# Head of an attention and spectral-convolution kernel: one load queue, other fillers, biases on ScalarE, keys of three blocks first, and the gate's means one step earlier

## The chip, the cores and the metric

The kernel runs on one core of a Trainium2 chip. The metric is the device time of one execution in microseconds (us). Three runs of the kernel before took 3039.53, 3043.44 and 3043.40 us; their median is 3043.4. A profile is one further execution, recorded by the hardware. The engines are named PE (TensorE; PEld is its weight load), DVE (VectorE), ACT (ScalarE), POOL (GpSimd) and SP (SyncE, which here only issues transfers).

## What is computed

The input x has four images of 64 channels and 96 x 96 pixels. Layer 0 is an attention over all 9216 pixels with a sigmoid in place of the softmax, followed by a channel gate; layer 1 mixes a few Fourier modes. Both stand behind a group normalisation and add to their input.

```python
q, k, v = wq @ g + bq, wk @ g + bk, wv @ g + bv      # g = _gn(x), 8, 8 and 64 channels
energy = einsum('bcn,bcm->bnm', q, k)
out = einsum('bcm,bnm->bcn', v, sigmoid(energy)) + g
scale = sigmoid(mlp(mean of out) + mlp(max of out))  # per image and channel
x = x + out * scale
x = x + irfft2(the 32 x 16 low modes of rfft2(_gn(x)), mixed over channels)
```

## The kernel before, in words

Two images share the 128 partitions, so there are two pairs of images, `x0` and `x1`, each a tile of 128 x 9216 numbers. A pair's pixels are cut into 18 blocks of 512. For each block of queries the kernel runs over 144 energy tiles of 128 x 512 (72 groups of 128 keys, two images). These are worked off in bursts of mostly seven: PE multiplies keys and queries into PSUM banks (`energies`, L531), ACT puts the sigmoid into one of two sets of seven slots of `at` (`sigmoids`, L552), and PE multiplies with the values into an accumulator bank (`attend`, L569). At the end of a block DVE adds the accumulator to x and takes its sum and maximum (L575, L577).

Before the first burst lies the head. Pair 0 is loaded in nine pieces of 1024 columns, 512 KB each, on the queues of SP (pieces 0, 2, 4, 6, 8) and ACT (1, 3, 5, 7), then constants and pair 1 follow on SP (L99 to L108). DVE takes statistics of each block (L583), aggregates them (L134), and a short chain over PE, DVE and POOL (`second` and `third` of `group_stats`, L136 to L149) gives the mean and the scale of each group. DVE normalises blocks 0 and 1 (L155). PE projects the keys of block 0 (L429), the queries (L519) and the values (L450). Keys and queries are split into a high part of fewer bits and a rest: DVE adds the bias out of PSUM (L435, L521), copies into the narrower type (L436, L522) and combines (L418). In between, `warm` (L622) issues products whose result nobody reads; some stand behind a statistic, some behind a projection.

What order the work has: in the head, a scheduler orders the instructions of each engine, with `issue_after` where an order is forced. From the first burst on, PE, ACT and DVE follow the program text (`manual_schedule`, L838). Which step stands beside which burst comes from a planner (L751 to L823): `together[t]` holds projections that share the banks of burst t + 1, `alone[t]` steps that stand by themselves, `ends[t]` steps for the end of burst t. Keys and values of later blocks of pair 0 are projected during the first bursts. A later block's query comes back from a copy of the split projections in DRAM (L493 stores, L510 loads, both on SP).

The last block of pair 0 has a crossing into the first block of pair 1. There, `second_layer(t)` (L676) plans layer 1 of pair 0, which runs beside the attention of pair 1. Its first step is the gate of pair 0: `means` (L598: three small DVE operations, L600 to L602, of which `f` comes out), `hidden` (L604: a PE product that reads `f`, L606) and `gates` (L609). Around the crossing the projections of pair 1 are made (`values_of(1, s)`), and their `rest` (L476) splits and turns queries and keys on DVE (L486, L487, L489).

Of the kernel before, what the change touches and what calls it, by code (L numbers as in the profile page):

```python
# [33 lines left out]
F32 = mybir.dt.float32  # L34
# [52 lines left out]
def tile_kernel(ctx: ExitStack, tc: tile.TileContext, x, cst, late, spec, out):  # L87
# [11 lines left out]
    for p in range(NPAIR):  # L99
        xt = xpool.tile([P, N], F32, tag=f"x{p}", name=f"x{p}")  # L100
        for s in range(9):
            cols = bass.ts(s, N // 9)
            queue = nc.scalar if p == 0 and s % 2 else nc.sync
            queue.dma_start(xt[:, cols], xf[bass.ts(p, P), cols])
        if p == 0:
            nc.sync.dma_start(cs[:, :NFIRST], cst[:, :NFIRST])
        xs.append(xt)
# [4 lines left out]
    def named(name, rows=P):  # L112
        return cs[:rows, PLACE[name]]
# [277 lines left out]
    with tc.tile_pool(name="work", bufs=1) as work, \  # L391
# [17 lines left out]
        def bank_a(name):  # L409
            return banks[:, spare[0], :]  # L410
# [5 lines left out]
        def low_or_high(dst, u, h, is_low):  # L416

            mark[0] = nc.vector.scalar_tensor_tensor(dst, h.bitcast(F32), is_low, u,  # L418
                                                     ALU.mult, ALU.add)

        def later(step):
            with tc.issue_after(mark[0].ins):
                step()

        def keys(p, s):
            pp = bank_a(f"pk_{p}_{s}")
            for e in range(2):
                cols = bass.ts(e, P // 2)
                projected[0] = nc.tensor.matmul(  # L429
                    pp[cols, :NB // 2], named("wk")[:, cols],  # L430
                    xs[p][:, bass.ts(2 * s + e, NB // 2)], start=True, stop=True)
            shape = [P, NB // 2]
            u = qp.tile(shape, F32, tag="turned", name=f"full_k_{p}_{s}")
            h = qp.tile(shape, F32R, tag="t", name=f"high_k_{p}_{s}", bufs=1)
            nc.vector.tensor_scalar(u, pp[:, :NB // 2], named("bk"), None, ALU.add)  # L435
            nc.vector.tensor_copy(h, u)  # L436
            low_or_high(kT[:, s, :, :], u.rearrange("p (m h) -> p h m", h=2),
                        h.rearrange("p (m h) -> p h m", h=2), low_sb[:, 1:2])

        def values_of(p, s, width=C + 2 * C8):  # L440


            pp = banks[:, spare[0]:spare[0] + 2, :].rearrange("p b (k m) -> p b k m", m=P)
            src = xs[p][:, bass.ts(s, NB)].rearrange("p (a m h) -> p a h m", a=2, h=2)
            for a in range(2):
                for h in range(2):
                    for e in range(2):
                        for b in range(2):
                            rows = bass.ts(b, C)
                            projected[0] = nc.tensor.matmul(  # L450
                                pp[bass.ts(e, P // 2), b, 2 * a + h, :width],
                                src[rows, a, h, bass.ts(e, P // 2)],
                                named("wv")[rows, :width], start=True, stop=True)

            def values():
                for b in range(2):
                    nc.vector.tensor_tensor(  # L457
                        vT[:, 4 * s:4 * s + 4, bass.ts(b, C)].rearrange(
                            "p (h a) m -> p a h m", h=2),
                        pp[:, b, :, :C].rearrange("p (a h) m -> p a h m", h=2),  # L460
                        named("bv")[:, :C].unsqueeze(1).unsqueeze(1).to_broadcast([P, 2, 2, C]),
                        ALU.add)

            if width == C:
                values()
                return None
            u = qp.tile([P, 2, 4, 2 * C8], F32, tag="u", name=f"u_{p}_{s}")
            nc.vector.tensor_tensor(
                u.rearrange("p b k o -> p (b k) o"),
                pp[:, :, :, C:width].rearrange("p b k o -> p (b k) o"),  # L470
                named("bqk").unsqueeze(1).to_broadcast([P, 8, 2 * C8]), ALU.add)
            values()

            k = 2 if p == 0 and s < DIRECT else 0

            def rest():  # L476
                t = qp.tile([P, 3, 2, 2, QK], F32R, tag="t", name=f"t_{p}_{s}", bufs=1)
                pieces = [(u[:, :, :, :C8],
                           t[:, 2].rearrange("p a h (b o l) -> p l b (a h) o", b=2, l=2))]
                if k == 0:  # L480
                    pieces += [(u[:, :, :, C8:].rearrange("p b k o -> p (b k) o").unsqueeze(3)
                                .to_broadcast([P, 8, C8, 2]),
                                t[:, :2].rearrange("p b a h (l o y) -> p l (b a h) o y",
                                                   l=2, y=2))]
                for whole, to in pieces:
                    nc.vector.tensor_copy(to[:, 0], whole)  # L486
                    nc.vector.tensor_tensor(to[:, 1], whole, to[:, 0].bitcast(F32), ALU.subtract)  # L487
                turned = qp.tile([P, 3, 2, NB // 8], F32, tag="turned", name=f"turned_{p}_{s}")
                nc.vector.transpose(  # L489
                    turned[:, k:].rearrange("p k a (m h) -> p (k a) h m", h=2),  # L490
                    t[:, k:].rearrange("p k a h m -> p (k a) h m").bitcast(F32))
# [23 lines left out]
        def first_queries():  # L515


            pq = bank_a("pq_first")
            projected[0] = nc.tensor.matmul(pq, named("wq"), xs[0][:, :NB], start=True, stop=True)  # L519
            qu, qh = at[:, 12, :], at[:, 13, :].bitcast(F32R)  # L520
            nc.vector.tensor_scalar(qu, pq, named("bq"), None, ALU.add)  # L521
            nc.vector.tensor_copy(qh, qu)  # L522
            q = qp.tile([P, NB], F32R, tag="q", name="q_first")
            low_or_high(q, qu, qh, low_sb[:, 0:1])
            return q

        def energies(t):

# [87 lines left out]

            return gate, [means, hidden, gates], f

        def warm(s, n=NB):


            return nc.tensor.matmul(banks[:, 7, :n], xs[0][:, s * NB:s * NB + P], xs[0][:, s * NB:s * NB + n],  # L622
                                    start=True, stop=True)

            if NBLK - 4 < s < NBLK:
                with tc.issue_after(last.ins):
                    warm(s, NB // 2)
        each, norm0, _ = stats_of(0)
        for s, step in enumerate(each):
            last = step()  # L630
            if s < NBLK:
                warm(s, NB // 2)
        with tc.issue_after(last.ins):
            warm(NBLK - 3)

        def warm_behind():
            with tc.issue_after(projected[0].ins):
                warm(NBLK - 1, NB // 2)

        norm0[0]()  # L640
        norm0[1]()
        spare[0] = 2
        keys(0, 0)
        warm_behind()
        spare[0] = 3
        q = first_queries()
        warm_behind()
        spare[0] = 0
        values_of(0, 0, C)
        warm_behind()  # L650

        together, alone, ends = {}, {}, {}

        def end(t, step):
            ends.setdefault(t, []).append(step)
# [20 lines left out]
        def second_layer(first):  # L676

            gate, steps, _ = after(0)
            end(first + 1, steps[0])
            for step in steps[1:]:  # L680
                follow(True, step, 2)
            l1 = Hidden(0, gate, bank_a, lambda dst, src: nc.vector.tensor_copy(dst, src), work)  # L682
# [46 lines left out]
        each, norm1, mv1 = stats_of(1)  # L729
        again = vT.rearrange("p j m -> p (j m)")  # L730
        kept = [TILES * (NPAIR * NBLK - 1) + 2 * (STRIP // P) * (s + 1) for s in range(NSTRIP)]
        ask, asked, known, valued, normal, renewed, again_at = {0: q}, 1, 2, 2, 3, 0, 0
        heads = [HEAD]
        sizes, total, order, done, block, edges = [5], [5], [[4, 5, 6, 3, 2]], [], [], set()
        way = 1
# [15 lines left out]
        while len(done) < len(sizes):  # L751
# [18 lines left out]
            elif total[t] < ALL:  # L770
# [2 lines left out]
                    steps.append((1, lambda s=known: keys(0, s)))  # L773
                    known += 1
                while (valued < min(NBLK, (total[t] + 5 * SIZE - 1) // 8 + 1)
                       and sum(n for n, _ in steps) <= 2):
                    steps.append((2, lambda s=valued: values_of(0, s)))
                    if valued >= DIRECT:
                        arrive(t, 0, valued)
                    valued += 1  # L780
# [47 lines left out]
        burst = [t for t, size in enumerate(sizes) for _ in range(size)]  # L828
        assert not chain and renewed == NBLK and asked == NPAIR * NBLK

        energies(0)
        sigmoids(0)
        later(norm0[2])
        spare[0] = 7
        keys(0, 1)
        spare[0] = 0
        values_of(0, 1)()
        with tc.manual_schedule(engines=ENGINES):  # L838
            put_off = []
            for t in range(T):  # L840
                if t + 1 < T:
# [305 lines left out]
```

## Time and profile before

| | |
|---|---|
| median of the runs | 3043.4 us |
| the profiled execution | 3040.91 us, of which the span of the trace is 3039.1 us |
| PE busy | 3014.8 us, 99% of the span |
| ACT busy | 2410.9 us, 79% |
| DVE busy | 309.0 us, 10% |
| first statistic starts, last one ends | 5.61 us, 17.11 us |
| first product of the mean chain (L138) starts | 17.84 us |
| first normalise starts | 20.39 us |
| first keys' product starts | 21.36 us |
| first energies start | 27.82 us |
| first sigmoid starts | 28.38 us |
| fourth burst's energies start | 41.46 us |
| queries of block 1 first used | 123.5 us |
| means of pair 0 (L600) start | 1494.95 us |

Times in the trace count from the span's start. In lines of a timeline the columns are start, length, engine, line of the program, operation, what is written and read, how many, and in brackets how long the engine stood idle before and what ended that. The lines of a table by stretches give, for each engine in turn (PE, PEld, DVE, ACT, POOL), its busy time and the number of instructions; then come the clock granted to PE as a share of full speed, the busy share of the DMA engines and the GB/s they moved. In the chain of work that ended last, each line is a start, a length and what ran.

### The profile page before, as it was taken

Reading aid. Unit: us, or ns where it says so; the run is one execution under the profiler, and the core shown is the slowest. Engines: PE = TensorE matmul, PEld = TensorE weight load, DVE = VectorE, ACT = ScalarE, POOL = GpSimd, SP = SyncE. Lnnn points to the kernel's source line nnn. Section 1 sums busy time; section 2 is a strip of 40 time slices with the busy share of each in tenths; the row PEclk is TensorE's granted clock in tenths of the full one; section 3 lists DMA queues with packets and bytes.
Section 4 is the critical chain, followed back from the end, with each engine's and each line's share of the span. In section 5 each row is a group of like instructions: output and inputs, shape, how many; then the busy total and the mean of one; then the engine's idle time right before and its main releaser. Section 6 shows DMA issues by size and latency. Waiting matters only on the chain.

```text
span 3039.1 us, 44084 instructions
## 1 busy us (share of the span) xinstructions
PE 3014.8 (99%) x19360; PEld 1112.5 (37%) x19360; DVE 309.0 (10%) x709; ACT 2410.9 (79%) x1541; POOL 75.5 (2%) x148
## 2 busy tenths in 40 slices
PE   8999999999999999999999999999999999999998
PEld 4333333333333333333333333333333333333335
DVE  6300000000000000002411101100000000000005
ACT  4788888888888888887788887777778888888872
POOL 0100000000000000001300000000001000000001
PEclk9999999999999999999999999999999999999999
DMA  4100000000000000001422322412113000000027
GB/s 158 32 4 4 4 4 4 4 4 4 1 4 4 4 4 4 4 4 34 95 68 67 87 78 86 134 33 45 52 45 121 4 4 4 4 4 5 5 62 252
DMA packets 114289, 117.34 MB, mean 39 GB/s; under 512 B 77520, under 2 KB 84432, under 8 KB 114000
## 3 DMA queue, kind: packets, MB, share of 16 engines
q1 hardware_dynamic: 103584, 86.20, 10.5%
q0 software_dynamic: 8848, 23.60, 2.4%
q10 hardware_dynamic: 1664, 4.72, 0.4%
q8 instruction: 152, 2.49, 0.3%
q14 instruction: 41, 0.34, 0.0%
HBM read 79.80 MB, written 33.49 MB: 37 GB/s over the span
## 4 chain that ended last, share of the span: by engine, by line
PE 97%; DVE 1%; DMA 1%; issue 0%; ACT 0%; POOL 0%; SPq 0%; DVEq 0%; POOLq 0%; ACTq 0%
PE banks L569 77%; PE banks L531 17%; PE banks L450 1%; PE banks L209 1%; PE pv L209 0%; DMA x<-in_x_dram 0%; PE pa L947 0%; DVE x L1052 0%; PE banks L382 0%; ACT at L552 0%; PE banks L429 0%; PE pu L959 0%; PE banks L305 0%; DMA vt<-vd 0%; PE pz L1031 0%
## 5 line engine op out<-in xcount | busy, mean ns | idle before, releaser
L552 ACT ACTIVATE at<-banks 128x2048 f32<-128x2048 f32 (+1 forms) x1501 | 2388.4, 1642 | 558.7 <-PE banks L531 543.9
L569 PE MATMUL banks<-at,vT 128*64 128x512 f32 (+1 forms) x11824 | 2400.8, 547 | 0.0
L569 PEld LDWEIGHTS banks<-at,vT 128*64 128x64 f32 x11824 | 778.3, 136 | 1361.5 <-issue 1306.5
L531 PE MATMUL banks<-q,kT 32*128 32x512 f32 x5040 | 541.8, 452 | 0.8 <-ACT at L552 0.7
L531 PEld LDWEIGHTS banks<-q,kT 32*128 32x128 f32 x5040 | 223.7, 183 | 446.3 <-issue 339.2
L575 DVE SCALAR_TENSOR_TENSOR x<-banks,x 128x512 f32<-128x512 f32 x36 | 24.9, 691 | 2022.0 <-PE banks L569 2022.0
L502 POOL DMA_DIRECT2D stage<-qk x96 | 47.6, 503 | 934.4 <-DMA qk<-turned 925.5
L386 DVE TENSOR_TENSOR x<-banks,x 128x768 f32<-128x768 f32 x12 | 11.5, 957 | 168.8 <-PE banks L382 153.2
L450 PEld LDWEIGHTS banks<-cs,x 64*64 64x64 f32 x1152 | 21.8, 135 | 16.2 <-ACT at L552 11.5
L457 DVE TENSOR_TENSOR vT<-banks,cs 128x256 f32<-128x256 f32 x72 | 26.8, 413 | 0.0
L450 PE MATMUL banks<-cs,x 64*64 64x80 f32 (+1 forms) x1152 | 25.9, 234 | 0.0
L577 DVE TENSOR_REDUCE maxs<-x 128x1 f32<-128x512 f32 x36 | 24.6, 684 | 1.2
L149 POOL TENSOR_TENSOR mr_l<-ve_l,cs 128x1 f32<-128x1 f32 x4 | 2.2, 561 | 841.1 <-DVE ve_l L148 841.1
L583 DVE BATCH_NORM_STATS2 stats<-x 128x6 f32<-128x512 f32 x36 | 22.2, 679 | 6.0 <-DMA x<-in_x_dram 5.9
L682 DVE COPY ws<-banks 128x512 f32<-128x512 f32 x16 | 11.1, 691 | 115.3 <-PE banks L209 115.3
L622 PE MATMUL banks<-x 128*128 128x256 f32 (+1 forms) x44 | 15.0, 486 | 6.3 <-DMA x<-in_x_dram 6.2
L682 DVE COPY ae<-banks 128x512 f32<-128x512 f32 x6 | 4.1, 692 | 157.6 <-issue 115.3
L932 POOL DMA_DIRECT2D x<-vT x3 | 2.7, 990 | 660.0 <-DVE less L922 660.0
L531 PE MATMUL banks<-q_first,kT 32*128 32x512 f32 x144 | 18.0, 459 | 0.9 <-ACT at L552 0.5
L489 DVE STREAM_TRANSPOSE turned<-t 128x384 f32<-128x384 f32 (+1 forms) x35 | 17.8, 510 | 1.2
L947 PE MATMUL pa<-xt,lc 128*128 128x256 f32 x72 | 16.9, 386 | 1.1 <-DVE xt L939 1.1
L155 DVE TENSOR_SCALAR x<-x,mr_l 128x512 f32<-128x512 f32 x36 | 17.7, 530 | 0.7 <-POOL mr_l L149 0.7
(135 smaller groups left out, 436.2 us busy)
## 6 DMA issues: line engine op xcount, KB each, us to landing
ws<-in_spec_dram SPq DMA_DIRECT2D x20, 512.0 KB
q<-qk SPq DMA_DIRECT2D x280, 32.0 KB
x<-in_x_dram SPq DMA_DIRECT2D x14, 512.0 KB
out_dram<-x SPq DMA_DIRECT2D x18, 384.0 KB
room<-in_spec_dram SPq DMA_DIRECT2D x12, 512.0 KB
w<-in_spec_dram POOLq DMA_DIRECT2D x10, 512.0 KB, 6.5
old<-in_x_dram SPq DMA_DIRECT2D x12, 384.0 KB
qk<-turned SPq DMA_DIRECT2D x96, 48.0 KB
```

The source lines that it names most:

```text
L155: nc.vector.tensor_scalar(dst, src, mr[:, 0:1], mr[:, 1:2], ALU.subtract, ALU.mult)
L209: self.last = nc.tensor.matmul(pv[bass.ts(g, 32), :].rearrange("q (n k o) -> q n k o", n=SIDE, o=C)[:, :, k, :], self.ut[:, at:at + 32], s ...
L450: projected[0] = nc.tensor.matmul(pp[bass.ts(e, P // 2), b, 2 * a + h, :width], src[rows, a, h, bass.ts(e, P // 2)], named("wv")[rows, :wi ...
L457: nc.vector.tensor_tensor(vT[:, 4 * s:4 * s + 4, bass.ts(b, C)].rearrange("p (h a) m -> p a h m", h=2), pp[:, b, :, :C].rearrange("p (a h) ...
L489: nc.vector.transpose(turned[:, k:].rearrange("p k a (m h) -> p (k a) h m", h=2), t[:, k:].rearrange("p k a h m -> p (k a) h m").bitcast(F32))
L502: nc.gpsimd.dma_start(come[bass.ts(r, QK), :], split[p][s][:, r % 2, bass.ts(r // 2, NB // 2)])
L531: nc.tensor.matmul(banks[:, bank_of(i), :], kT[r:r + 32, i % TILES // 8, i // 4 % 2, :], ask[i // TILES][r:r + 32, :], start=True, stop=True)
L552: nc.scalar.activation(at[:, of:of + n, :], banks[:, bank:bank + n, :], AF.Sigmoid)
L569: attended[0] = nc.tensor.matmul(acc[half, cols], vT[:, j, half], at[:, place(2 * pair + b), cols], start=(j == 0), stop=(j == NCH - 1 and ...
L575: nc.vector.scalar_tensor_tensor(blk, acc, 1.0, blk, ALU.mult, ALU.add, accum_out=sums[p][:, m:m + 1])
L577: mark[0] = nc.vector.tensor_reduce(maxs[p][:, m:m + 1], blk, AX.X, ALU.max)
L583: each = [lambda s=s: nc.vector.bn_stats(stats[:, s, :], xs[p][:, bass.ts(s, NB)]) for s in range(NBLK)]
```

## The change

The load of pair 0 uses SP's queue alone, and its last piece is split in two. An instruction list shows ten transfers of pair 0 on SP, then the constants and pair 1; ACT's queue is empty and ACT starts with the sigmoid's table.

The head is now ordered by the program text on PE, ACT and DVE. `warm` stands ahead of each statistic, three more follow the last one, one stands between the two products of the mean chain, and two follow the second. None stands between the projections. In PE's list there are 21 unused products, the first mean product, one unused, the second mean product, two unused (512 and 256 columns), then keys 0, queries, keys 1 and 2, values 0, energies, values 1, energies.

Three blocks are normalised before the projections, not two. The biases of the queries and of the keys of blocks 0 to 2 are added by ACT (`both`). Keys 1 and 2 are projected into the two halves of one bank, and split on DVE behind the eviction of values 0. Before, keys 1 and 2 were projected and split between the first bursts. Keys 3 and later are as before.

At the crossing, `means` is planned for the end of burst `first`, not `first + 1`; DVE's list has its three operations ahead of the evictions of blocks 16 and 17 and their splitting, not behind.

SP's list differs in two more places: four of the eight loads of block 1's queries, and two strips of layer 1's fetch, stand behind stores of the second and the fourth block of split projections. POOL's list is the same. From the fourth burst on PE's list is the same.

```diff
         for s in range(9):
-            cols = bass.ts(s, N // 9)
-            queue = nc.scalar if p == 0 and s % 2 else nc.sync
-            queue.dma_start(xt[:, cols], xf[bass.ts(p, P), cols])
+            parts = 2 if p == 0 and s == 8 else 1
+            for i in range(parts):
+                cols = bass.ts(parts * s + i, N // 9 // parts)
+                nc.sync.dma_start(xt[:, cols], xf[bass.ts(p, P), cols])
...
-        def keys(p, s):
-            pp = bank_a(f"pk_{p}_{s}")
+        def key_matmuls(p, s, side=0):
+            pp = bank_a(f"pk_{p}_{s}")[:, bass.ts(side, NB // 2)]
...
+        def key_splits(p, s, pp, ahead=False):
...
+            if ahead:
+                both(u, h, pp, named("bk"))
+            else:
+                nc.vector.tensor_scalar(u, pp, named("bk"), None, ALU.add)
+                nc.vector.tensor_copy(h, u)
...
+        def both(u, h, pp, bias):
+
+            nc.scalar.activation(u, pp, AF.Identity, bias=bias)
+            nc.vector.tensor_copy(h, u)
+
+        def keys(p, s):
+            key_splits(p, s, key_matmuls(p, s))
...
+        table = small.tile([P, 1], F32, tag="t", name="table")
+        nc.vector.memset(table, 0.0)
+        nc.scalar.activation(table, table, AF.Sigmoid)
         each, norm0, _ = stats_of(0)
-        for s, step in enumerate(each):
-            last = step()
-            if s < NBLK:
-                warm(s, NB // 2)
-        with tc.issue_after(last.ins):
-            warm(NBLK - 3)
...
-        norm0[0]()
-        norm0[1]()
-        spare[0] = 2
-        keys(0, 0)
-        warm_behind()
-        spare[0] = 3
-        q = first_queries()
-        warm_behind()
-        spare[0] = 0
-        values_of(0, 0, C)
-        warm_behind()
+        with tc.manual_schedule(engines=ENGINES):
+            for s, step in enumerate(each):
+                if s < NBLK:
+                    warm(s)
+                step()
+                if s == NBLK - 1:
+                    for _ in range(3):
+                        warm(NBLK - 1)
+                if s == NBLK + 1:
+                    warm(NBLK - 1)
+            warm(NBLK - 1, NB)
+            warm(NBLK - 1)
+            for s in range(3):
+                norm0[s]()
+            spare[0] = 2
+            first_keys = key_matmuls(0, 0)
+            key_splits(0, 0, first_keys, True)
+            spare[0] = 3
+            q, split_queries = first_queries()
+            spare[0] = 7
+            next_keys = [key_matmuls(0, s, s - 1) for s in (1, 2)]
+            spare[0] = 0
+            first_values = values_of(0, 0, C)
+            split_queries()
+            first_values()
+            for s in (1, 2):
+                key_splits(0, s, next_keys[s - 1], True)
...
             gate, steps, _ = after(0)
-            end(first + 1, steps[0])
+            end(first, steps[0])
...
-        ask, asked, known, valued, normal, renewed, again_at = {0: q}, 1, 2, 2, 3, 0, 0
+        ask, asked, known, valued, normal, renewed, again_at = {0: q}, 1, 3, 2, 3, 0, 0
...
-                       and sum(n for n, _ in steps) <= 2):
+                       and sum(n for n, _ in steps) <= min(2, t + 1)):
...
-        energies(0)
-        sigmoids(0)
-        later(norm0[2])
-        spare[0] = 7
-        keys(0, 1)
-        spare[0] = 0
-        values_of(0, 1)()
         with tc.manual_schedule(engines=ENGINES):
+            energies(0)
+            sigmoids(0)
+            spare[0] = 0
+            values_of(0, 1)()
             put_off = []
```

More of the change, by code (lines that the diff above doesn't have):

```diff
@@ L419, in low_or_high @@
                                                      ALU.mult, ALU.add)
-        def later(step):
-            with tc.issue_after(mark[0].ins):
-                step()
-        def keys(p, s):
-            pp = bank_a(f"pk_{p}_{s}")
+        def key_matmuls(p, s, side=0):
+            pp = bank_a(f"pk_{p}_{s}")[:, bass.ts(side, NB // 2)]
             for e in range(2):
@@ L429, in keys @@
                 projected[0] = nc.tensor.matmul(
-                    pp[cols, :NB // 2], named("wk")[:, cols],
+                    pp[cols, :], named("wk")[:, cols],
                     xs[p][:, bass.ts(2 * s + e, NB // 2)], start=True, stop=True)
+            return pp
+        def key_splits(p, s, pp, ahead=False):
             shape = [P, NB // 2]
@@ L434, in keys @@
             h = qp.tile(shape, F32R, tag="t", name=f"high_k_{p}_{s}", bufs=1)
-            nc.vector.tensor_scalar(u, pp[:, :NB // 2], named("bk"), None, ALU.add)
-            nc.vector.tensor_copy(h, u)
+            if ahead:
[3 more added lines that the diff above has]
+                nc.vector.tensor_copy(h, u)
             low_or_high(kT[:, s, :, :], u.rearrange("p (m h) -> p h m", h=2),
                         h.rearrange("p (m h) -> p h m", h=2), low_sb[:, 1:2])
+        def both(u, h, pp, bias):
[3 more added lines that the diff above has]
+            key_splits(p, s, key_matmuls(p, s))
         def values_of(p, s, width=C + 2 * C8):
@@ L464, in values_of @@
             if width == C:
-                values()
-                return None
+                return values
             u = qp.tile([P, 2, 4, 2 * C8], F32, tag="u", name=f"u_{p}_{s}")
@@ L519, in first_queries, with splits @@
             projected[0] = nc.tensor.matmul(pq, named("wq"), xs[0][:, :NB], start=True, stop=True)
-            qu, qh = at[:, 12, :], at[:, 13, :].bitcast(F32R)
-            nc.vector.tensor_scalar(qu, pq, named("bq"), None, ALU.add)
-            nc.vector.tensor_copy(qh, qu)
             q = qp.tile([P, NB], F32R, tag="q", name="q_first")
-            low_or_high(q, qu, qh, low_sb[:, 0:1])
-            return q
+            def splits():
+                qu, qh = at[:, 12, :], at[:, 13, :].bitcast(F32R)
+                both(qu, qh, pq, named("bq"))
+                low_or_high(q, qu, qh, low_sb[:, 0:1])
+            return q, splits
         def energies(t):
@@ L617, in after @@
             return gate, [means, hidden, gates], f
[L619 to L625, printed above, removed]
-                with tc.issue_after(last.ins):
-                    warm(s, NB // 2)
-        each, norm0, _ = stats_of(0)
-        for s, step in enumerate(each):
-            last = step()
-            if s < NBLK:
-                warm(s, NB // 2)
@@ L633, in tile_kernel, with warm @@
-        with tc.issue_after(last.ins):
-            warm(NBLK - 3)
-        def warm_behind():
-            with tc.issue_after(projected[0].ins):
-                warm(NBLK - 1, NB // 2)
-        norm0[0]()
-        norm0[1]()
-        spare[0] = 2
-        keys(0, 0)
-        warm_behind()
-        spare[0] = 3
-        q = first_queries()
-        warm_behind()
-        spare[0] = 0
-        values_of(0, 0, C)
-        warm_behind()
+        def warm(s, n=NB // 2):
+            nc.tensor.matmul(banks[:, 7, :n], xs[0][:, s * NB:s * NB + P], xs[0][:, s * NB:s * NB + n],
+                             start=True, stop=True)
```

## The prediction, made before the changed kernel ran

> **What bounds the kernel now.** I first read the page's chain of work that ended last.
>
> ```profile
> PE 97%; DVE 1%; DMA 1%; issue 0%; ACT 0%; POOL 0%; SPq 0%; DVEq 0%; POOLq 0%; ACTq 0%
> ```
>
> TensorE (PE) is the bound almost everywhere, so only the stretches in which it waits, or does work that nobody uses, can give time. The list of PE's own waits after 28 us has one large entry, 2.8 us for `f` at L606; the next are 0.5 to 1.1 us. By the busy time of short stretches PE has no gap from 38 us on until there. So two places matter: the head, and the crossing from pair 0 to pair 1 near 1493 us. For the head I read the same chain piece by piece (start us, us, what).
>
> ```profile
> 2.12 11.31 DMA x<-in_x_dram
> 13.45 3.67 DVE stats L583 x6
> ...
> 18.93 0.59 PE banks L146 x2
> 19.52 1.92 PE banks L622 x2
> 21.43 1.05 PE banks L429 x4
> 22.48 1.15 PE banks L622 x2
> 23.64 1.71 PE banks L519 x2
> 25.34 0.70 PE banks L622 x2
> 26.05 0.64 PE banks L450 x32
> 26.69 0.63 PE banks L622 x2
> 27.32 0.58 PE banks L429 x2
> ```
>
> The load ends, six statistics follow, then a chain in which the unused L622 products take 4.4 us. The granted clock in the same stretches (the number behind the POOL column):
>
> ```profile
> 18.00:20.00 2.00, 1.30 (x5) 1.07 (x6) 0.69 (x4) 0.00 (x0) 0.20 (x1) 0.73 1.01 401
> 20.00:22.00 2.00, 2.00 (x6) 0.30 (x4) 1.00 (x2) 0.00 (x0) 0.36 (x1) 0.50 1.05 420
> 22.00:24.00 2.00, 2.00 (x7) 1.18 (x4) 1.26 (x3) 0.00 (x0) 0.00 (x0) 0.50 1.01 401
> 26.00:28.00 2.00, 2.00 (x41) 1.22 (x41) 1.93 (x6) 0.00 (x0) 0.00 (x0) 1.00 0.78 309
> ```
>
> PE runs at half clock just while keys and queries are projected. The crossing, from the timeline:
>
> ```profile
> 1491.54 1.01 PE L531 MATMUL banks<-q,kT 32*128 32x512 f32 x6
> 1494.44 0.58 DVE L489 STREAM_TRANSPOSE turned<-t 128x384 f32<-128x384 f32 x1
> 1495.18 0.16 DVE L602 TENSOR_REDUCE f<-maxs 128x1 f32<-128x18 f32 x1
> 1495.40 0.20 PE L606 MATMUL banks<-f,cs 128*8 128x2 f32 x2 [2.84 <-DVE f L602]
> ```
>
> The means sit on DVE behind the splitting of two blocks; PE, in order, stands still for 2.84 us.
>
> **What the Trainium skill says.** "TensorE: Matmul & The Clock Gate", section "What's actually happening": half clock after a mostly idle window of about 3.4 us, full after a busy one. The trace agrees on the drop (PE idle 1.51 and 0.70 us before the two mean products, then 0.50); the recovery near 25.5 us took some 6 us of modelled business, longer than the page has. "DMA: Bandwidth & Descriptors", section "Issuing engines are not separate DMA queues": both queues run on the same 16 engines. Trace: 410 to 430 GB/s with two queues (3 to 10 us), 400 to 420 with SP's alone (14 to 24 us). "ScalarE: Activation LUTs", section "Table sets: the hidden batching unit": identity is in every set. Only a sigmoid load (1.28 us at 3.09) is seen here; the changed program also lists one load. Price for a bias on ScalarE, same page, "What ACT_TABLE_LOAD costs": 280 ns + 0.833 ns per element.
>
> **The change, part by part.**
>
> *Load over one queue.* An x piece is 524 KB. Before, pieces arrive in twos, one of each queue: DVE starts at 5.61, the next waits end near 8.3, 10.9 and 13.4. By the bandwidth rows 192 KB moved in the first 3 us and some 415 KB/us after, so 1049 KB are across at 5.06: 0.55 us from the last byte to the consumer. In one queue, piece 0 is across at 3.0 + 332/415 = 3.8 and seen at 4.35; all 4719 KB at 13.9, seen at 14.5 to 14.7. I take 14.6. DVE needs 18 x 0.61 = 11.0 us from 4.35, about the pace of arrival; the last statistic, half a piece, ends at 14.6 + 0.68 = 15.3, against 17.12. Up to eight transfers are under way in both programs, so the queue doesn't run dry. Unknown is the single queue's start: at best as above, at worst the half rate each queue had while sharing (rival 4). ScalarE loses four issues (2.3 us) that delayed nobody. The constants, 314 KB behind x, land about 15.4, ahead of their use.
>
> *Unused products.* The last statistic's product and three more go behind the last piece: 4 x 0.43 (two passes of 256 columns at full clock) hold PE till 16.3. The aggregate is ready at 15.3 + 0.64 + 0.04 = 16.0, so the mean product starts at 16.3, not 17.84: **-1.5 us**. These 0.3 us are the price of keeping the clock. Of the following, one lies between the two mean products and 1.3 us behind the second, under the 0.9 us to the end of POOL's power and 0.5 of the first normalise. The next steps take what they took (17.84 to 20.39 = 2.55): normalise at 18.85, projections from 19.4. The 0.9 to 1.9 us of L622 between keys, queries and values go.
>
> *Keys of three blocks, biases on ScalarE, one more normalise.* At full clock PE needs 0.6 for two key products (0.60 at 33.61), 0.9 for queries, 1.2 for four more key products, 0.7 for values: 19.4 to 22.8. Beside it ScalarE adds the key bias (0.49) at 20.05 and the query bias (0.28 + 427 ns = 0.71) at 20.9 to 21.65. On DVE the same biases cost 0.48 and 0.75 (L435, L521), so ScalarE is no faster; it frees DVE for the third normalise (till 20.3). DVE's cast and combination of the query: 0.43 + 0.75 to 22.9. First energies at 22.95 instead of 27.82; 1.5 of that is counted, so **-3.4 us**. ScalarE's price is bounded by 0.4 (256 elements at the sigmoid rows' 0.83 ns each and their fixed 0.17) and 1.0 us: 0.4 us either way. Added waits: the third bias waits for a buffer that the first combination frees at 21.4; the first sigmoid queues behind it, but it ends at 22.7, before the energies.
>
> *Splits ahead.* Before, the third energies stall: the chain above goes on at 34.33 with bias, cast and combination of block 2, and these energies run 34.86 to 37.08. Ready keys make them wait only for sigmoids and for the values' eviction. Counted from the first sigmoid: eviction of values 1 after 2.7 us (two splits, 1.6, now stand ahead of it on DVE, bounded by sigmoids of 3.9 us anyway), values 2 out at 6.7, third energies' products done at 7.15 instead of 8.6: **-1.45 us** (bounds 0 and 2.2, the whole stretch less 0.73 of work). Next late is PE itself.
>
> *Moved DMAs.* On SP the first four query loads pass behind the second block's stores, two strip loads behind the second four. The queries are used at 123.5 us, the strips at 1503: 80 us of cover. POOL's order is the same.
>
> *Means ahead.* L600 to L602 follow the key copies (DVE free at 1487.6, next busy 1490.19): `f` by 1488.1. PE goes on at 1492.6; its next 12 products read sigmoids that ended at 1490.3. ScalarE's next short piece waited 1.16 us behind the first of these; now it waits for ScalarE (1494.06) and ends at 1495.1, ahead of the next energies at 1495.4. **-2.8 us** (bounds 1.5 and 2.84).
>
> Sum: 1.5 + 3.4 + 1.45 + 2.8 = **9.1 us**. The profiled execution took 3040.9 (span 3039.1 and 1.8 around it): 3031.8. The median shown is 2.5 higher: 3034.3. I forecast 3033, between them. What a measurement tells from no change is about 0.2%, 6.1 us.
>
> **Rivals.**
> 1. *The crossing gap only changes its owner* (ScalarE's next piece, or keys from POOL's transfers). For: ScalarE waits 2.62 us for PE there. Against: its wait ends with PE's products. Head alone: 6.3 us less, 3036.
> 2. *The clock falls anyway.* For: PE's duty in the load drops to two products of 0.43 per 1.28 us and the mean chain stays thin. At half clock projections take 1.2 + 1.9 + 2.2 + 1.4 = 6.7 us, ending at 26.1: 3.1 us lost, 3036.
> 3. *Arrival gives nothing*, DVE starting again at 5.6: 1.3 us lost, 3034.5.
> 4. *Slower: one queue carries only the half rate, 205 GB/s, that each had while two shared.* Then x is seen at 3.0 + 4527/205 + 0.55 = 25.6, 11 us after my 14.6, and the balance is 1.9 us slower, 3044. It decides below 4527/(23.7 - 3.55) = 225 GB/s. Against: pair 1's pieces, on SP alone, at 408.
>
> **Chances.** Forecast 0.60 (own range 3029 to 3037), rival 1 0.12, rival 2 0.11, rival 3 0.13, rival 4 0.04. Low end: all bounds at their good side (10.5 us) from the profiled time, less 2 for scatter. High end: 5 us from the median, which takes in rivals 1 to 3 and a little scatter. Faster by over 0.2%: most of forecast and rival 3, half of 1 and 2, 0.80; within 0.17; slower 0.03.
>
> **What would show it.** First statistic near 4.4, last over by 15.4; mean product at 16.3; clock 1.00 throughout; projections from 19.4 to 22.8; first sigmoid near 23.5; third energies about 7 us later without a wait for `kT`; L606 without 2.8 us ahead of it. A first statistic at 5.6 or a last beyond 17, clock 0.5 after 18, or a new PE gap near 1493 would make it wrong.

## The result, and the profile after

| | before | after |
|---|---|---|
| median of 17 runs each | 3042.7 us (3039.5 to 3047.0) | 3035.9 us (3033.0 to 3041.3) |
| ratio, 95% interval | | 0.998 (0.9973 to 0.9986) |
| profiled execution (span) | 3040.9 us (3039.1) | 3037.6 us (3035.8) |

The change takes 6.8 us at the medians, 0.2%, where the sum had 9.1. The forecast of 3033 was 2.9 us too low, and the time lies in the range of 3029 to 3037. The two profiled executions differ by only 3.3 us. Where that comes from is seen by cutting both traces at the same steps (us, from the starts of PE's instructions; the fourth burst is the first that lies behind all of the head's special order):

| piece | before | after | difference |
|---|---|---|---|
| start to first energies | 27.82 | 23.53 | -4.29 |
| first to fourth burst's energies | 13.64 | 13.94 | +0.30 |
| fourth burst to the crossing | 1450.08 | 1450.73 | +0.65 |
| crossing burst | 6.71 | 3.79 | -2.92 |
| second half | 1452.78 | 1453.08 | +0.30 |
| tail, from the last energies | 88.11 | 90.74 | +2.63 |

The page's chain of work that ended last has the same first entry as before:

```profile
PE 97%; DVE 1%; DMA 1%; ACT 0%; issue 0%; POOL 0%; DVEq 0%; ACTq 0%; POOLq 0%
```

PE is still the bound, and "SPq" is gone from the list. PE's own waits in the changed kernel (what waited, for whom: us in total, times, longest):

```profile
PE banks L633 <- DMA x<-in_x_dram: 4.7, 1, 4.7
PE pz L1044 <- DMA vt<-vd: 2.1, 1, 2.1
PE banks L542 <- ACT at L563: 1.8, 3, 1.1
```

Of the two waits for `f`, the one of 2.8 us is gone; the other, 0.6 us at the same step at the end of pair 1, is left (L617 is the former L606). Longer than before are the waits for sigmoids (L563; the longest 1.1 us, 0.5 before) and the one for `vt` in the tail, the stretch behind the last energies (2.1 us, 0.6 before). Next, the timeline of the head of the changed kernel, the lines that answer to the prediction's steps:

```profile
4.71 11.40 DVE L594 BATCH_NORM_STATS2 stats<-x 128x6 f32<-128x512 f32 x18 [3.84 <-DMA x<-in_x_dram]
16.86 0.37 PE L139 MATMUL banks<-mv_l,cs 128*128 128x1 f32 x2
19.19 1.46 DVE L156 TENSOR_SCALAR x<-x,mr_l 128x512 f32<-128x512 f32 x3 [0.68 <-POOL mr_l L150]
20.49 0.47 ACT L445 ACTIVATE full_k<-banks,cs 128x256 f32<-128x256 f32 x1 [18.26 <-PE banks L426]
21.54 0.69 ACT L445 ACTIVATE at<-banks,cs 128x512 f32<-128x512 f32 x1 [0.57 <-PE banks L529]
23.53 0.73 PE L542 MATMUL banks<-q_first,kT 32*128 32x512 f32 x5 [0.37 <-DVE q_first L419]
26.04 1.17 PE L542 MATMUL banks<-q_first,kT 32*128 32x512 f32 x7 [1.07 <-ACT at L563]
27.15 3.57 PE L580 MATMUL banks<-at,vT 128*64 128x512 f32 x8
37.47 0.77 PE L542 MATMUL banks<-q_first,kT 32*128 32x512 f32 x7
```

The 18 statistics run in one piece, the mean product starts 0.98 us earlier than before, and the first energies 4.29 us earlier. Then the energies wait 1.07 us for a sigmoid, and the first eight products with values take 3.57 us. In the timeline of the kernel before, the same eight took 1.94:

```profile
31.84 1.94 PE L569 MATMUL banks<-at,vT 128*64 128x512 f32 x8
```

The table by stretches of the changed kernel says why (the clock stands behind the POOL column):

```profile
20.00:22.00 2.00, 2.00 (x12) 0.72 (x10) 1.43 (x4) 0.94 (x2) 0.00 (x0) 1.00 1.02 408
24.00:26.00 2.00, 0.97 (x37) 0.63 (x32) 1.83 (x7) 1.89 (x2) 0.00 (x0) 1.00 1.02 408
26.00:28.00 2.00, 1.96 (x9) 0.85 (x11) 1.29 (x5) 1.89 (x3) 0.00 (x0) 0.76 0.75 291
28.00:30.00 2.00, 2.00 (x8) 0.48 (x4) 0.00 (x0) 1.81 (x2) 0.00 (x0) 0.50 0.22 49
```

The projections now run at full clock. Behind them PE is busy for 0.97 us of two, and the clock falls to 0.50 from about 27 to 30.5. So the fall has moved: from the projections to the first burst with values. The crossing, in the timeline of the changed kernel:

```profile
1484.43 0.16 DVE L613 TENSOR_REDUCE f<-maxs 128x1 f32<-128x18 f32 x1
...
1488.19 1.00 PE L542 MATMUL banks<-q,kT 32*128 32x512 f32 x6
1489.13 0.20 PE L617 MATMUL banks<-f,cs 128*8 128x2 f32 x2
1489.25 2.79 PE L580 MATMUL banks<-at,vT 128*64 128x512 f32 x12
```

`f` is there 4.5 us ahead of its reader, and PE goes from energies through the gate's product into values without a gap.

### The profile page after: what moved, and what is told of

Its sections match the earlier page's. It is cut to its first block, busy times and chain, and to the rows that moved or that the text cites. A ratio compares the mean times of both kernels' runs of the same rounds, so it can differ in the third digit from the quotient of the medians.

```text
span 3035.8 us, 44098 instructions
## 1 busy us (share of the span) xinstructions
PE 3015.8 (99%) x19364; PEld 1113.1 (37%) x19364; DVE 307.3 (10%) x706; ACT 2413.0 (79%) x1546; POOL 75.2 (2%) x148
## 3 DMA queue, kind: packets, MB, share of 16 engines
q1 hardware_dynamic: 104304, 88.29, 10.5%
## 4 chain that ended last, share of the span: by engine, by line
PE 97%; DVE 1%; DMA 1%; ACT 0%; issue 0%; POOL 0%; DVEq 0%; ACTq 0%; POOLq 0%
PE banks L580 77%; PE banks L542 17%; PE banks L461 1%; PE banks L210 1%; PE banks L633 0%; PE pa L960 0%; DVE x L1065 0%; PE banks L383 0%; ACT at L563 0%; DMA vd<-vm 0%; DMA vt<-vd 0%; PE pz L1044 0%; PE pu L972 0%; PE banks L306 0%; PE banks L426 0%
## 5 line engine op out<-in xcount | busy, mean ns | idle before, releaser
L563 ACT ACTIVATE at<-banks 128x2048 f32<-128x2048 f32 (+1 forms) x1501 | 2388.3, 1642 | 533.7 <-PE banks L542 521.8
```

The lines of the kernel that those rows point to most:

```text
L563: nc.scalar.activation(at[:, of:of + n, :], banks[:, bank:bank + n, :], AF.Sigmoid)
```

## The experiments

**The theory:** the ready keys gave nothing in the profile because PE, with its waits for the query (0.37 us) and for a sigmoid (1.07 us), becomes too idle in 24 to 27 and loses its clock for about 3.4 us. **Rivals:** the waits of the new order themselves cost the 1.4 us; or ready keys were never worth it, whatever the clock. For the change as a whole, another question was how much of the 4.29 us belongs to the kernels and how much to the executions.

### Two unused products in the gap

```diff
             values_of(0, 1)()
+            for _ in range(2):
+                warm(NBLK - 1)
             put_off = []
```

> The changed kernel with two unused products of 256 columns behind values 1, in PE's gap ahead of the second energies (24.93 to 26.04 us). Theory (the missing 2.3 us of the head are the clock: PE is too idle from 23 to 26 us, the granted clock falls at 27 and the first eight attention products take 3.57 us, not 1.94): clock 1.00 from 26 to 32 us, these products in 1.94, fourth energies at 35.8 instead of 37.47, total about 1.6 us under the changed kernel. Rival (the first products are slow because ScalarE and DVE work beside them, or the third energies wait for sigmoids anyway): the same 3.5 us, fourth energies at 37.5, or full clock but fourth energies within 0.3 of 37.5.

The timeline and the stretches of this kernel:

```profile
26.06 1.15 PE L542 MATMUL banks<-q_first,kT 32*128 32x512 f32 x7
27.14 1.94 PE L580 MATMUL banks<-at,vT 128*64 128x512 f32 x8
...
35.83 0.77 PE L542 MATMUL banks<-q_first,kT 32*128 32x512 f32 x7
```

```profile
26.00:28.00 2.00, 2.00 (x12) 0.90 (x13) 1.30 (x5) 1.88 (x4) 0.00 (x0) 1.00 0.82 320
```

The second energies start at the same time as in the changed kernel (26.06 against 26.04), so the products fit in the wait. The clock stays at 1.00, the eight products take 1.94 us, and the fourth burst's energies come at 35.83, 1.64 us earlier. From first to fourth energies it is now 12.28 us against 13.64 before the change. Ready keys do save 1.36 us, where the prediction said 1.45; the waits as such do not cost it, the clock did. The whole time, 3035.2 us in the median of ten (3032.9 to 3036.6; ratio to before 0.9976, interval 0.9967 to 0.9986), can't be told from the changed kernel's 0.998. The profiled execution gave 0.7 us of the gain back in the tail (91.43 us against 90.74), and its span is 1.0 us shorter (3034.8 against 3035.8).

### Four unused products

```diff
             split_queries()
+            warm(NBLK - 1)
             first_values()
...
             values_of(0, 1)()
+            for _ in range(3):
+                warm(NBLK - 1)
```

In this kernel the keys of block 1 are taken from the unused product, which stands in their bank.

> As before it, with one more unused product ahead of the first energies, and three instead of two behind values 1. Theory: full clock too; the fourth product makes the second energies up to 0.2 us later than with two, so fourth energies at 35.8 to 36.1. If two were too few and four are enough, the fall of the clock depends on how much of the window is filled: 3.57 there, 1.94 here. Rival: 3.5 us in both.

First energies 23.95, second 26.82, fourth 36.31; the clock stays at 1.00; one time, 3033.4. In this execution the mean product starts 0.22 us later than with two (17.10 against 16.88), ahead of anything in which the two programs differ. Counted from it, the first energies come 0.2 us later than with two, the second 0.5 and the fourth 0.3. So more products than the gap holds push the energies back, the second by more than the 0.2 us expected.

### The means alone, on the kernel before

```diff
-            end(first + 1, steps[0])
+            end(first, steps[0])
```

> The kernel before with the means planned one step earlier and nothing else. Theory (the crossing's share is by itself): head as before, fourth energies at 41.46, no wait of 2.84 us at L606, and energies after the crossing 2.9 us earlier than before (1498.25 to about 1495.3). Rival (the earlier head made part of it): under 2.5 us.

The crossing in this kernel's timeline:

```profile
1489.57 0.20 PE L606 MATMUL banks<-f,cs 128*8 128x2 f32 x2
1489.70 2.80 PE L569 MATMUL banks<-at,vT 128*64 128x512 f32 x12
```

There is no gap at L606; the burst takes 3.79 us instead of 6.71, which is 2.92, all of it by this one line. The surprise is in the head, whose program is that of the kernel before. There the stretch that had half clock before now reads:

```profile
20.00:22.00 2.00, 1.49 (x8) 0.88 (x8) 1.67 (x4) 0.00 (x0) 0.00 (x0) 1.00 1.03 410
```

Full clock, and first energies at 24.93 instead of 27.82. The fall at the projections, which the prediction took for a property of the kernel before, is not in every execution. One time, 3035.9.

### The load over two queues again

```diff
-                nc.sync.dma_start(xt[:, cols], xf[bass.ts(p, P), cols])
+                queue = nc.scalar if p == 0 and s % 2 else nc.sync
+                queue.dma_start(xt[:, cols], xf[bass.ts(p, P), cols])
```

> The changed kernel with pair 0 loaded over two queues again (ACT issues every second piece; the last piece is still in two halves). Theory (DVE's own pace sets the end of the statistics, so one queue is worth only the earlier first piece): first statistic at 5.6 instead of 4.71, last over at 17.0 to 17.2 instead of 16.11, everything behind 0.9 to 1.0 us later, fourth energies at 38.4. Rival (arrival sets it): the last statistic waits for the last half piece, and the difference is 1.5 us or more, or below 0.5 if the half piece on the other queue arrives as early.

The first statistics and the mean product in this kernel's timeline:

```profile
5.64 11.35 DVE L595 BATCH_NORM_STATS2 stats<-x 128x6 f32<-128x512 f32 x18 [4.77 <-DMA x<-in_x_dram]
17.73 0.38 PE L140 MATMUL banks<-mv_l,cs 128*128 128x1 f32 x2 [0.22 <-DVE mv_l L136]
```

The first piece arrives 0.93 us later than over one queue, the mean product starts 0.87 later, and the first energies come at 24.41, 0.88 later. By this pair one queue is worth 0.9 us, and all of it is the earlier first piece; over either, DVE runs the 18 statistics at 0.63 us without a pause. In all profiles together the first statistic starts at 4.43 to 4.92 us over one queue (eight) and at 5.57 to 5.64 over two (four).

But the clock did not fall in this profile, although PE had the same wait for the sigmoid (1.08 us). To compare the two one needs the stretch ahead of the fall. In every trace the changes of the granted clock lie whole multiples of 3.413 us apart; in the changed kernel's, for example, it falls at 27.05 us, comes back at 30.46 and falls again 873 multiples later, at 3010.30. So a trace can be cut into windows of 3.413 us: the changed kernel's by these falls, this one's by its only fall, at 3029.45, behind PE's last product. The changed kernel's window ahead of its fall reads, in its table by stretches:

```profile
23.63:27.05 3.42, 2.35 (x44) 1.37 (x44) 3.18 (x12) 2.83 (x3) 0.00 (x0) 1.00 1.02 405
```

The two-queue kernel's window with the wait reads, in its table:

```profile
25.72:29.13 3.41, 2.33 (x21) 1.04 (x15) 2.31 (x9) 3.29 (x4) 0.00 (x0) 1.00 0.57 223
```

PE is busy for 2.35 us of the one and 2.33 of the other, and only behind the first did the clock fall. This speaks against the theory in its simple form: the waits make a fall possible and do not force it. The fourth energies (36.69) stand 0.86 us behind those with two unused products, the load's share again.

### The changed kernel again, and the kernel before again

Both without an edit.

> The changed kernel once more. Theory (whether the clock falls at 27 us differs between executions of one program): the profile either repeats the fall (0.50 at 28 us, fourth energies at 37.5) or, as in the run with two queues, has none (fourth energies at 35.8); of the timed executions some have a mean clock of 0.998 and some of 0.999 or 1.0, and the former take 1.5 to 3 us longer. Rival (the fall belongs to the program): it repeats in the profile, and the mean clock is the same in all.

> The kernel before once more. Theory (its fall at 19 us is not in every execution): first energies at 27.8 with the fall or at 24.9 without it, as in the run with the means alone. Rival (the means' edit changed the head): first energies at 27.8.

The changed kernel fell again at the same place, in its stretches:

```profile
28.00:30.00 2.00, 2.00 (x8) 0.47 (x4) 0.00 (x0) 1.55 (x1) 0.00 (x0) 0.60 0.21 47
```

First energies 23.27, fourth 37.04. Its seven times have a median of 3034.1 us (3032.8 to 3038.3; ratio 0.9971, interval 0.996 to 0.9983). Their mean clocks differ, as the theory had it: five have 0.999 or 1.0, and the two with 0.998 are the slowest (3037.6 and 3038.3). The kernel before had its first energies at 26.55 this time, a third value for one program, and its crossing became worse. First its timeline, then its table by stretches:

```profile
1494.13 0.20 PE L606 MATMUL banks<-f,cs 128*8 128x2 f32 x2 [2.84 <-DVE f L602]
1494.26 4.49 PE L569 MATMUL banks<-at,vT 128*64 128x512 f32 x12
```

```profile
1496.00:1498.00 2.00, 2.00 (x8) 0.49 (x4) 0.00 (x0) 0.54 (x1) 1.28 (x3) 0.50 0.47 78
```

Behind the same 2.84 us gap the clock fell, and twelve products took 4.49 us where they take 2.79. So the gap costs 2.9 us in one profile and 4.6 in the other (8.40 less 3.79), and closing it takes away both. Here, too, the windows of 3.413 us differ between the executions. In the repeat 2.4 us of the gap lie in the window ahead of the fall (1491.70 to 1495.11; PE busy for 0.98 us). In the first profile a boundary at 1493.50 cuts it, and PE is busy for 2.46 us of the window on the one side and 1.51 of that on the other.

### Keys 1 and 2 between the bursts again

```diff
-            spare[0] = 7
-            next_keys = [key_matmuls(0, s, s - 1) for s in (1, 2)]
...
-            for s in (1, 2):
-                key_splits(0, s, next_keys[s - 1], True)
...
             sigmoids(0)
+            spare[0] = 7
+            keys(0, 1)
             spare[0] = 0
```

The planner's two conditions go back to what they were as well (`known` 2, at most 2 steps).

> The changed kernel with the keys of blocks 1 and 2 projected and split between the first bursts again, on DVE, as before; load, fillers, ScalarE's biases for block 0 and the queries stay. Theory (ready keys are worth 1.4 us at full clock, from the 13.64 us between first and fourth energies before against 12.28 with two fillers): first energies at 23.5, fourth at 37.1 to 37.3 with the clock at 1.00, since the key products fill PE's gap. Rival (ready keys are worth nothing, sigmoids and the values' eviction bind): fourth energies at 35.8 to 36.1 at full clock.

The first and the fourth energies in this kernel's timeline:

```profile
23.26 0.73 PE L542 MATMUL banks<-q_first,kT 32*128 32x512 f32 x5 [1.39 <-DVE q_first L419]
...
36.92 0.77 PE L542 MATMUL banks<-q_first,kT 32*128 32x512 f32 x7
```

From the one to the other it takes 13.66 us, the 13.64 of before, at full clock: the key products of block 1 stand in the very gap in which the changed kernel has nothing to do. With ready keys it is 12.28 where the clock holds and 13.94 or 13.77 where it falls. So moving the keys ahead took 1.38 us of work and waits off this stretch, took the filling out of the gap with it, and the stretch came out 0.1 and 0.3 us longer in the two profiles of the changed kernel.

### The biases on DVE

```diff
-            nc.scalar.activation(u, pp, AF.Identity, bias=bias)
+            nc.vector.tensor_scalar(u, pp, bias, None, ALU.add)
```

> The changed kernel with the four biases of the head on DVE instead of ScalarE. Theory (ScalarE's part is to take 0.48 and 0.75 us off DVE's queue): first energies about 0.4 us later than 23.53 (bias, cast and combination of block 0 and of the queries follow the third normalise one after another), eviction of values 1 about 1.4 later, and fourth energies 1.0 to 1.5 us later than at the same clock with ScalarE (35.8 at full clock, 37.5 with a fall). Rival (ScalarE's 0.47 and 0.69 us are no shorter, nothing is won): first and fourth energies within 0.2 us.

First energies 23.86 against 23.53: ScalarE's biases are worth 0.33 us up to there. On DVE everything behind is later, too: the eviction of values 1 ends at 27.69 instead of 26.65 (1.0 us later; 1.4 were expected). The clock falls for 6.8 us instead of 3.4 (eight products 3.68 us), and the fourth energies come at 39.27, 1.8 us behind the changed kernel. How much of the 1.8 the biases cause and how much chance does, one profile can't say.

### Without the products in the mean chain

The six unused products behind the last statistic (three, one between the two mean products, two behind them) are left out.

```diff
-                if s == NBLK - 1:
-                    for _ in range(3):
-                        warm(NBLK - 1)
-                if s == NBLK + 1:
-                    warm(NBLK - 1)
-            warm(NBLK - 1, NB)
-            warm(NBLK - 1)
```

> The changed kernel without the six unused products behind the last statistic (three ahead of the mean chain, one in it, two behind it); the 18 beside the statistics stay. Theory (they hold the clock through the projections): PE is idle from 16 to 19.7 us but for the two mean products, the granted clock falls to 0.50 between 19 and 22 us, and the first energies come 1.3 to 3 us later than 23.5. Rival (18 products beside the statistics are enough, or the window lies well): clock 1.00 to 24 us and first energies at 23.2 to 23.5, the mean product starting at 16.8 as with them, since DVE's aggregate ends then.

The projections in this kernel's table by stretches:

```profile
22.00:24.00 2.00, 2.00 (x20) 0.86 (x21) 1.18 (x2) 0.78 (x2) 0.00 (x0) 0.50 1.05 418
```

PE now idles in the mean chain (busy 0.46 us between 18 and 20, 1.92 in the changed kernel) and projects keys 1 and 2 and values 0 at half clock, as the profiled kernel before projected keys and queries. The mean product starts at 16.98 instead of 16.86, so these products cost no wait; without them the first energies come 1.2 us later (24.75), a little less than the 1.3 to 3 expected. The clock falls a second time at 28, and the fourth energies come at 38.86.

### Two unused products, and one more in the tail

Two unused products as in the first experiment, and one more for PE ahead of its wait for `vt` in the tail:

```diff
-        occupy(9, l1.last, mix_bank)
+        occupy(10, l1.last, mix_bank)
```

> The kernel with two fillers, and ten instead of nine unused products ahead of the last wait for vt in the tail. In ten profiles PE waited there 0.38 to 2.32 us, and where it waited 1.5 us or more the products behind took 6.3 us, not 4.66, in five of six cases. Theory (those are falls of the clock, which a wait shorter by 0.9 us avoids): fourth energies at 35.5 to 35.9, products in 4.66 us, and total 0.5 to 1 us under the changed kernel with two fillers, at 0.997 of the kernel before. Rival (the later transfer itself slows them): 6.3 us after long waits still, no gain in total.

The products that read `vt`, in this kernel's timeline:

```profile
3007.04 4.66 PE L1046 MATMUL pz<-vt,gh_in_fours 64*128 64x256 f32 x32 [0.26 <-DMA vt<-vd]
```

In the timeline of the changed kernel the line of the same products is:

```profile
3009.73 6.32 PE L1044 MATMUL pz<-vt,gh_in_fours 64*128 64x256 f32 x32 [2.05 <-DMA vt<-vd]
```

The products are as short as the theory had it, but one profile doesn't test the theory: with nine products ahead of the wait, executions that waited 0.38 or 0.45 us had 4.66 as well. The median of eight is 3033.3 us (3032.7 to 3034.4), the lowest median here, and the ratio to before 0.9972 (0.9962 to 0.9983). Its interval overlaps those of the changed kernel and of the kernel with two products, so "faster" is not shown. What stands out is the spread: 1.6 us from the lowest to the highest of eight, where the kernel with two products has 3.7 in ten, and the changed kernel 8.3 in 17 and 5.5 in the seven of its repeat. The fourth energies stand at 35.82, as with the two products alone (35.83).

## Why the prediction was nearly right, and where it was not

**Load and statistics: -1.5 predicted, -0.98 in the profile.** The mechanism holds: one queue delivers the first piece early (4.71; predicted 4.35), and the rate is not halved, so the slower rival fell. "DMA: Bandwidth & Descriptors", as cited in the prediction, agrees: 373 to 438 GB/s during the load with SP's queue alone. What was mis-sized is the start and the pace: 0.36 us later, and 0.633 us for each of 18 statistics, not 0.61, so the last ends at 16.11, not 15.3. The "0.3 us that are the price of keeping the clock" did not occur: the aggregate ended at 16.79, after the unused products.

**Mean chain and projections: -3.4 predicted, -3.3 in the profile (4.29 less 0.98), but not for the reason given.** The chain from the mean product to the first normalise takes 2.33 us (before 2.55), from there to the energies 4.34 (I had 4.1). ScalarE's biases take 0.47 and 0.69 us; 0.49 and 0.71 came from the price in "ScalarE: Activation LUTs", so the trace agrees. But I set this against a head whose fall is not in every execution. The three profiles with the head of before give 27.82, 26.55 and 24.93, mean 26.4; against these the head gains 4.3, 3.0 or 1.4 us. My "-3.4" was right as a difference from one profile and not a property of the edit; that it came so near was luck.

**Splits ahead: -1.45 predicted, +0.30 in the profile.** This is the step that failed. The sum behind it is right: 1.36 us at full clock. What failed is the sentence "Next late is PE itself" and, with it, "clock 1.00 throughout". I took the work out of PE's way and did not ask what else PE had to do while it waited for a sigmoid. The clock fell in both profiles of the changed kernel, and the eight products and their neighbours took back 1.7 us (13.94 less 12.28). Rival 2 had the clock falling, but at the projections, where the unused products held it (without them it fell there). My upper bound of 2.2 for this step was wrong as well: the stretch that I named, 34.86 to 37.08, less 0.73 of work is 1.5. The good sides then add up to 9.6 us and not 10.5; the low end of the range stays 3029.

**Moved DMAs: nothing predicted,** and no wait for a query or a strip is in the list of PE's waits.

**Means ahead: -2.8 predicted, -2.92 measured,** in the changed kernel and alone. It is the safest part of the change. In the repeat of the kernel before, where the clock fell behind the gap, it cost 1.7 us more.

**The balance.** Head to the fourth energies: the changed kernel has 37.47 and 37.04; the head of before 41.46, 40.18 and 38.57, mean 40.1. That is some 2.8 us of gain on the means of these few profiles. With 2.9 at the crossing, or more where the clock falls there, and a loss of about 0.6 on the way to it (below), it comes to some 5 us or a little more; the medians say 6.8. The tail scatters by over 3 us between profiles of all these kernels, so this is as near as landmarks come. The 2.3 us by which my sum was too large is of the size of the clock's 1.7 and the load's 0.5, but the landmarks don't add up closely enough to show that these are the whole of it.

**Left open.** All kernels with the new head lose 0.2 to 0.8 us between the fourth burst and the crossing (1450.26 to 1450.84, against 1450.06 to 1450.11), 0.62 of it in two small steps near 846 and 1090 us in the profiled pair. The order of bursts and banks is the same in both programs there. The two steps stand in all seven profiles with four biases of the head on ScalarE, and in neither of the two with fewer (keys between the bursts, biases on DVE), which lose 0.2 and 0.3 us in all; why is not known. Open as well is why the two-queue kernel, with the same waits, kept its clock. PE's busy share of a window doesn't decide it (0.68 against 0.69 in the changed kernel). The windows hold different products: the changed kernel's energies and value projections, the two-queue kernel's some of the attention's products with values, too. Whether that counts is not shown.

## What to carry to other kernels

When a change clears waits and work off the head of an engine with a granted clock, look in the table by stretches for what is left in the gaps: a gap of 1.1 us that nothing fills can cost 1.7 us behind it, and two unused products that fit inside it held the clock in both profiles that had them. Price a step at full clock and at half clock before counting it, and take a second profile before a fall in one execution is counted as a property of the program: where the windows of the clock lie against a gap differs between executions. For changes of a few us compare the starts of the same instruction in several traces, since the totals carry the chance falls of every other stage.

## What was not expected of the hardware

- "TensorE: Matmul & The Clock Gate", section "What's actually happening", as cited in the prediction, has half clock after an idle window of about 3.4 us ("mostly" is the prediction's word). Here the clock also fell where PE was far from idle: busy for 0.69 of the changed kernel's window, longest wait 1.07 us. While PE has work, a fall lasts 3.41 or 6.83 us, which agrees with the page's window. In the twelve traces every fall follows a window in which PE was busy for 0.74 or less, and no window with 0.75 or more was followed by one. Below that it went either way: 0.74, 0.69 and 0.58 were followed by a fall in the head; 0.68, 0.64 and 0.60 were not, nor was 0.44 at the crossing. (PE's busy time is modelled.) Among profiles with nothing in the gap before the second energies four of five fell (the changed kernel twice, the biases on DVE, no chain products; not the two-queue kernel); of the four with products in it (two, four, two and the tail's, keys between) none did, nor in the three with the head of before, which has key products there.
- In the tail, waits for `vt` of 0.26 to 1.51 us left the next 32 products at 4.66 us in seven profiles; waits of 1.50 to 2.32 us made them 6.32 to 6.35 in five.
- Executions of one kernel order by the mean clock granted over the whole run: of the changed kernel's 17, two at 1.000 had a median of 3033.4 us, nine at 0.999 3035.7, six at 0.998 3037.8. A thousandth of the span is 3 us, and a fall of 3.4 us to half clock takes 1.7 of it.
